# Two-layer graph attention on one core: a scores group, a combination group and the multiplications with the inverses change their places

## The chip, the cores and the metric

The kernel runs on one core of a Trainium2 chip. The metric is the device time of one launch in microseconds (us), a median of runs. A core has five engines, each with its own queue of instructions: the matrix engine (PE), the vector engine (DVE), the scalar engine (ACT), GpSimd (POOL) and the sync engine (SP), which here only issues transfers (DMA). The engines run beside each other and wait for each other by semaphores. PE writes its results to the accumulation memory PSUM[...]; DVE and ACT read them from there.

## The reference, cut to what matters

64 graphs of 256 nodes with 512 features go through two layers. Each layer normalises, applies ReLU and masked multi-head attention, and adds the result to its input.

```python
# layer 0: 4 heads of 64 (Wq, Wk, Wv, Wo), adj masks the scores
h = relu(layernorm(x));  x = x + attention0(h, adj)
# layer 1: layernorm once more inside, 8 heads of 64 (w_qkv, w_out), mask = adj | eye
h = relu(layernorm(x));  x = x + attention1(layernorm(h) * gamma + beta, adj)
# attention: softmax(where(mask, q k^T / 8, very negative)) v, then the output projection and a bias
```

All is in float32.

## The kernel before

`fast_path` takes the graphs two at a time: 32 steps, each with 512 rows (NT = 4 tiles of 128 rows). A head pair (two heads of 64, 128 columns) of one layer is a **unit**; layer 0 has the units (0,0) and (0,1), layer 1 has (1,0) to (1,3). Layer 1 takes them in the order 0, 2, 1, 3.

What one unit does, with the lines that the profile names:

- **scores** (PE, L742): q k^T, transposed, for two heads and two graphs into four PSUM tiles `sc`. DVE adds the mask (L750), which also frees the PSUM tile; ACT takes the exponential (L751); POOL adds the two halves of the keys (L752).
- **weigh** (PE, L763): the exponentials times v into one `sc` tile `po`, and the sums of the exponentials (L773) into another. DVE takes the reciprocal of the sums (L778, two instructions), and SP spreads the inverses over the partitions with eight transfers (L784). `inv` and `invb` have one buffer each.
- **normalise** (DVE): `po` times the inverses (L799), and a check of the range (L800). These two free the tiles `po` and `sums`.

The pool of `sc` tiles has four buffers. So a scores group, which takes all four, waits for the L799 and L800 of the weighing before it, and a weighing that directly follows a scores group waits for the first two L750 of that group. The pool `mm` for all other PE results has four buffers as well.

Around the units lie the projections: q and k (L654; `project_qk`, by seven products of half size instead of eight, evacuated in `evacuate` by L598 to L610), v of layer 0 (`project_v0`, L678, four groups, evacuated by ACT's L682) and v of layer 1 (L692). `combine0` (L703, four groups, added to x by DVE's L707) and `combine1` (L717, seven groups, evacuated in `accumulate` by L617 to L632, with POOL's L620, L621 and L626) are the output projections. `norm1` takes row statistics (L523, L524), the negative mean (L563), ReLU on ACT (L564) and the statistics of that; `norm0` takes the statistics of layer 0's input; `row_scales` makes the scale (POOL L531) and shift (DVE L532) from them. `transpose_h` turns a normalised tile on PE (L581), evacuated by ACT (L585 in layer 0, L587 in layer 1); `act_sums` forms the four sums that the seven products need on POOL (L396 to L399). The load of the next h (L467) has one buffer and follows the transposes of the h before it.

**The order.** Steps are laid over each other: in one period PE does layer 1 of step s, the middle of step s+1 and the projections of layer 0 of step s+2. Every piece of work is entered with a time by hand, `at(period, place, ...)`; a period is 6.1 of these units. The pieces are then recorded in the order of their times. On PE this recorded order is the program's order (`manual_schedule` for PE alone). The order of the instructions on DVE, ACT, POOL and SP is set by a scheduler at build time, which takes the recorded order as one of its inputs. [...]

`attend` enters a unit: its scores at `place`, its weighing at `weighed` (plus a thousandth), its normalise some time later.

Of the kernel before, what the change touches and what calls it, by code (L numbers as in the profile page):

```python
# [315 lines left out]
def fast_path(  # L316
# [498 lines left out]
    def at(period, place, fn, *args):  # L815
        events.append((period * PERIOD + place, len(events), fn, args))

    def at_set(period, place, share, fn, *args):
        for i, n in enumerate((1, 6, 7, 5, 2, 4, 3)):
            at(period, place + i * share / 7, fn, *args, n)  # L820

    def attend(period, place, s, lyr, pr, later, weighed, first, last):

        at(period, place, scores, s, lyr, pr)
        at(period + later, weighed + 0.001, weigh, s, lyr, pr)
        at(period + later, weighed + 0.3, normalise, s, lyr, pr, first, last)

    for s in range(NSTEP):

        p = s - 2  # L830
        at(p - 1, 5.7, load_h, s)
        at(p, 0.2, adjacency_cast, s)
        for t in range(NT):
            at(p, 0.4 + 0.4 * t, norm0, s, t)
            at(p, 2.05 + 0.2 * t, scale_row, s, t)
        at(p, 2.4, adjacency_turn, s)
        at(p, 2.75, masks, s)
        for c in range(NC):
            at(p, 3.03 + 0.03 * c, transpose_h, s, 0, c)
        at_set(p, 3.57, 1.0, project_qk, s, 0, 0)  # L840
        for t in range(NT):
            at(p, 4.57 + 0.14 * t, project_v0, s, t)
        attend(p, 4.85, s, 0, 0, 0, 5.7, True, False)
        attend(p, 5.7, s, 0, 1, 1, 1.0, False, True)
        p = s - 1
        at(p, 1.4, load_x, s)
        at(p, 2.6, first_bias, s)
        for t in range(NT):
            at(p, 3.0 + 0.14 * t, combine0, s, t)
            at(p, 3.5 + 0.25 * t, norm1, s, t)  # L850
            at(p, 4.5 + 0.1 * t, scale_row, s, t)

        for c in range(NC):
            at(p, 5.13 + 0.02 * c, transpose_h, s, 1, c)
        p = s
        at_set(p, 0.0, 1.0, project_qk, s, 1, 0)
        at_set(p, 1.0, 1.0, project_v1, s)
        at_set(p, 2.0, 1.0, project_qk, s, 1, 1)
        attend(p, 1.0, s, 1, 0, 0, 2.1, True, False)
        attend(p, 2.1, s, 1, 2, 0, 3.0, False, False)  # L860
        attend(p, 3.0, s, 1, 1, 0, 3.6, False, False)
        attend(p, 3.6, s, 1, 3, 0, 4.2, False, True)
        at_set(p, 5.2, 0.9, combine1, s)
        at(p, 6.1, store, s)
# [12 lines left out]
def kernel(tc, *args):  # L877
    nc = tc.nc
    B, N, _ = args[0].shape
    P = 128  # L880
    with tc.tile_pool(name="guard", bufs=1) as guard:
        extremes = guard.tile([P, B // 2 * 6], FP, name="extremes")
        ident = guard.tile([P, P], FP, name="ident")
        make_identity(nc, ident)
        fast_path(tc, *args, ident, extremes)
        safe = guard.tile([1, 1], I32, name="safe")
        with tc.tile_pool(name="gps", bufs=1, space=bass.MemoryType.PSUM) as ps:
            top = guard.tile([P, 1], FP, name="top")
            nc.vector.tensor_reduce(top, extremes, axis=mybir.AxisListType.X, op=ALU.max)
            row = ps.tile([1, P], FP, name="row")  # L890
            nc.tensor.transpose(row, top, ident)
            all_top = guard.tile([1, 1], FP, name="all_top")
            nc.vector.tensor_reduce(all_top, row, axis=mybir.AxisListType.X, op=ALU.max)
            nc.vector.tensor_scalar(safe, all_top, LIMIT, None, op0=ALU.is_le)
        flag = nc.values_load(safe[0:1, 0:1], min_val=0, max_val=1, skip_runtime_bounds_check_because="a comparison gives 0 or 1")
        with tc.If(flag < 1):
            general_path(tc, *args)
# [29 lines left out]
```

## Time and profile before

| | |
|---|---|
| time, median of 3 runs | 3617.09 us (3614.64 to 3617.94) |
| profiled execution, span on the core | 3612.3 us |
| granted TensorE clock, mean | 0.989 |
| bytes moved by DMA | 165.45 MB, 46 GB/s in the mean |
| inverses, L784 | 1536 transfers of 32 KB, 1.8 us each from issue to landing |
| DVE waits for the inverses (L799) | 546.3 us in 165 waits |

The page sums the busy time of each engine and gives its share of the span. Since instructions of different engines overlap, these shares don't add up to anything; what counts is which engine is hardly ever idle, and what it waited for when it was. In a list of waits each line names who waited, for whom, and then the total, the number and the longest of the waits in microseconds. In a timeline each line gives the start, the length, the engine, the source line, the operation, output and input tiles and the number of merged instructions; a bracket at the end gives the idle time before it and what ended it. Matmuls in float32 appear twice per instruction of the program: 16 records of L742 are one scores group of 8.

### The profile page before, as it was taken

What the parts mean: (1) busy time and instruction counts of PE and PEld (TensorE: products, weight loads), DVE (VectorE), ACT (ScalarE), POOL (GpSimd) and SP (SyncE); (2) the same over time, 40 slices, a digit from 0 to 9 for tenths busy, and PEclk for the clock granted to TensorE, in tenths of its full rate; (3) what the DMA queues carried; (4) which work ended last, traced back from release to release, by engine and by line L of the source; (5) the groups of instructions that cost most, each with busy time, mean ns of one, the idle gap of its engine ahead of it and who ended that gap; (6) DMA issues with size and microseconds to landing.
All of it is one profiled execution on the core that took longest, in us unless ns stands there. A gap on an engine that the chain in (4) does not pass through costs nothing.

```text
span 3612.3 us, 51508 instructions
## 1 busy us (share of the span) xinstructions
PE 3473.9 (96%) x19555; PEld 2653.3 (73%) x19586; DVE 2068.4 (57%) x3873; ACT 1146.8 (32%) x1873; POOL 1652.7 (46%) x1387
## 2 busy tenths in 40 slices
PE   5999999999999999999999999999999999999987
PEld 4777777777777777777777777777777777777765
DVE  4555565565565556555566555565655565655553
ACT  2333333333332333232333333333333332333321
POOL 4445444454444455444545444544444554445432
PEclk8999999999999999999999999999999999999998
DMA  4011111111111111111111111111111111111100
GB/s 134 24 49 52 28 42 50 50 51 33 44 45 50 49 51 29 42 49 52 50 52 29 42 50 50 52 38 42 40 51 50 50 30 42 49 50 50 39 27 24
DMA packets 146956, 165.45 MB, mean 46 GB/s; under 512 B 43272, under 2 KB 94992, under 8 KB 146704
## 3 DMA queue, kind: packets, MB, share of 16 engines
q1 hardware_dynamic: 141312, 155.30, 14.1%
q10 hardware_dynamic: 5392, 6.82, 0.6%
q8 instruction: 155, 2.54, 0.3%
q14 instruction: 97, 0.79, 0.1%
HBM read 78.12 MB, written 33.55 MB: 31 GB/s over the span
## 4 chain that ended last, share of the span: by engine, by line
PE 67%; DVE 12%; DMA 8%; SPq 8%; issue 2%; ACT 1%; POOL 0%; DVEq 0%; POOLq 0%
PE mm L654 23%; PE mm L692 11%; SPq L784 8%; PE sc L742 8%; PE sc L763 7%; PE mm L703 5%; PE mm L717 5%; DMA h<-in_x_dram 4%; DMA invb<-inv 4%; DVE inv L778 3%; PE mm L678 3%; DVE bs L523 2%; PE sc L773 2%; DVE p L750 2%; PE mm L581 2%
## 5 line engine op out<-in xcount | busy, mean ns | idle before, releaser
L752 POOL TENSOR_TENSOR pd<-p 128x512 f32<-128x512 f32 x384 | 479.0, 1269 | 777.5 <-PE sc L773 732.8
L654 PE MATMUL mm<-hT,wqkv 128*128 128x256 f32 x3584 | 804.3, 381 | 1.6
L654 PEld LDWEIGHTS mm<-hT,wqkv 128*128 128x128 f32 x3584 | 676.0, 190 | 105.7 <-issue 13.5
L751 ACT ACTIVATE p<-p 128x512 f32<-128x512 f32 x768 | 464.1, 630 | 572.4 <-DVE p L750 570.5
L750 DVE TENSOR_TENSOR p<-sc,n 128x512 f32<-128x512 f32 x768 | 481.0, 680 | 154.7 <-PE sc L742 150.0
L742 PE MATMUL sc<-qk 64*128 64x256 f32 x3072 | 415.1, 395 | 34.6 <-DVE oT L799 25.9
L799 DVE TENSOR_TENSOR oT<-sc,invb 128x512 f32<-128x512 f32 x192 | 132.6, 691 | 547.2 <-DMA invb<-inv 546.3
L717 PE MATMUL mm<-wo,oT 128*128 128x256 f32 x1792 | 405.5, 384 | 18.5 <-POOL oT L397 13.1
L654 PE MATMUL mm<-hT,wqk 128*128 128x256 f32 x1792 | 409.0, 383 | 1.2 <-issue 1.2
L763 PE MATMUL sc<-p,v 128*64 128x256 f32 x3072 | 375.5, 386 | 29.3 <-DVE p L750 26.9
L692 PE MATMUL mm<-wqkv,hT 128*128 128x256 f32 x1792 | 400.6, 381 | 0.0
L654 PEld LDWEIGHTS mm<-hT,wqk 128*128 128x128 f32 x1792 | 335.8, 190 | 82.9 <-issue 40.8
L742 PEld LDWEIGHTS sc<-qk 64*128 64x128 f32 x3072 | 287.4, 187 | 148.0 <-issue 63.1
L717 PEld LDWEIGHTS mm<-wo,oT 128*128 128x128 f32 x1792 | 338.6, 192 | 76.6 <-POOL oT L397 14.2
L778 DVE RECIPROCAL inv<-sc 128x128 f32<-128x128 f32 x384 | 338.8, 923 | 83.3 <-PE sc L773 79.9
L692 PEld LDWEIGHTS mm<-wqkv,hT 128*128 128x128 f32 x1792 | 338.0, 190 | 57.6 <-issue 13.1
L480 POOL TENSOR_TENSOR xt<-xt,bo_b 128x512 f32<-128x512 f32 x128 | 161.4, 1292 | 466.1 <-DMA xt<-in_x_dram 327.9
L763 PEld LDWEIGHTS sc<-p,v 128*64 128x64 f32 x3072 | 211.2, 137 | 187.1 <-DVE p L750 83.0
L703 PE MATMUL mm<-wo,oT 128*128 128x512 f32 x512 | 235.8, 603 | 19.5 <-DVE oT L799 19.5
L538 ACT ACTIVATE h<-h,mr,r 128x512 f32<-128x512 f32 x256 | 187.5, 802 | 208.4 <-DVE mr L532 208.4
L678 PE MATMUL mm<-wv,hT 128*128 128x256 f32 x1024 | 243.9, 393 | 0.0
L523 DVE BATCH_NORM_STATS2 bs<-h 128x6 f32<-128x512 f32 x256 | 171.3, 680 | 99.3 <-ACT h L564 54.7
(105 smaller groups left out, 3375.7 us busy)
## 6 DMA issues: line engine op xcount, KB each, us to landing
invb<-inv SPq DMA_DIRECT2D x1536, 32.0 KB, 1.8
h<-in_x_dram SPq DMA_DIRECT2D x32, 1024.0 KB, 5.1
xt<-in_x_dram SPq DMA_DIRECT2D x32, 1024.0 KB, 5.1
out_dram<-xt SPq DMA_DIRECT2D x32, 1024.0 KB, 4.3
ad<-in_adj_dram SPq DMA_DIRECT2D x32, 128.0 KB, 2.2
wr<-in_L_gnn_w_qkv_dram ACTq DMA_DIRECT2D x3, 1024.0 KB, 8.2
wr<-in_L_gnn_w_out_dram ACTq DMA_DIRECT2D x1, 1024.0 KB, 8.7
wqk<-in_L_gnn_Wq_dram ACTq DMA_DIRECT2D x4, 128.0 KB, 4.9
```

The costliest lines, as they stand in the source:

```text
L654: nc.tensor.matmul(bank[:, k, :], w[:, wa, c, k, a * P:(a + 1) * P], st["hT"][:, ba, c, :], start=first and (k, c) == (0, 0), stop=(k, c) ...
L678: nc.tensor.matmul(bank, st["hT"][:, b0 + t // NIC * step, c % HC, i:i + P], wv0[:, c, :], start=(c == 0), stop=(c == NC - 1),)
L692: nc.tensor.matmul(bank[:, t, :], st["hT"][:, ba, c, t * P:(t + 1) * P], wqkv1[:, wa, c, 2, :], start=first and (t, c) == (0, 0), stop=(t, ...
L703: nc.tensor.matmul(bank, st["oT0"][:, pr, t // NIC, t % NIC * P:(t % NIC + 1) * P], wo0[:, pr, :], start=(pr == 0), stop=(pr == PR0 - 1),)
L717: nc.tensor.matmul(bank[:, t, :], st["oT1"][:, ba, c, t * P:(t + 1) * P], wo1[:, wa, c, :], start=first and (t, c) == (0, 0), stop=(t, c) ...
L742: nc.tensor.matmul(sc[e, g][:, kc, :], qk[rows, 1, k0:k0 + P], qk[rows, 0, g * N:(g + 1) * N], start=True, stop=True,)
L750: nc.vector.tensor_tensor(p[e][:, g], sc[e, g], neg[:, :, g, :], ALU.add)
L751: nc.scalar.activation(p[e][:, g], p[e][:, g], AF.Exp, scale=SCALE)
L752: nc.gpsimd.tensor_tensor(pd[:, e], p[e][:, :, 0, :], p[e][:, :, 1, :], ALU.add)
L763: nc.tensor.matmul(po[e * DH:(e + 1) * DH, g, :], st[f"v{lyr}"][:, g * NIC + kc, c0:c0 + DH], p[e][:, g, kc, :], start=(kc == 0), stop=(kc ...
L778: nc.vector.reciprocal(inv[:, i * P:(i + 1) * P], sums[:, i * P:(i + 1) * P])
L784: nc.sync.dma_start(invb[d0:d0 + 32, g, :], inv[r0:r0 + 32, :])
```

## The change

Three kinds of places move.

- The scores of unit (0,0) are entered at 5.0 instead of 4.85. The four groups of `project_v0` stand at 4.57, 4.71, 4.85 and 4.99, so the scores now follow all four; before they stood between the third and the fourth (in some early steps between the second and the third). The weighing of (0,0) and the scores of (0,1) go from 5.7 to 5.75, and thereby behind the fifth group of `combine1` (5.714) instead of the fourth. This is meant to give the L799 of unit (1,3), which frees two of the `sc` tiles, more time.
- The first group of `combine0` is entered at 3.01 instead of 3.0, and thereby behind the weighing of unit (1,2) at 3.001. Before it stood between the scores of (1,1) and that weighing. The three other groups follow after the transposes, as before. This is meant to bring that weighing and its inverses forward.
- `normalise` is entered 0.5 behind its weighing instead of 0.3, except for the last unit of a layer in a step. This is meant to let other DVE work go ahead of a multiplication that would have to wait for its inverses.

The same instructions are executed with the same operands.

```diff
@@ attend
         at(period, place, scores, s, lyr, pr)
         at(period + later, weighed + 0.001, weigh, s, lyr, pr)
-        at(period + later, weighed + 0.3, normalise, s, lyr, pr, first, last)
+        at(period + later, weighed + (0.3 if last else 0.5), normalise, s, lyr, pr, first, last)
@@ for s in range(NSTEP), p = s - 2
             at(p, 4.57 + 0.14 * t, project_v0, s, t)
-        attend(p, 4.85, s, 0, 0, 0, 5.7, True, False)
-        attend(p, 5.7, s, 0, 1, 1, 1.0, False, True)
+        attend(p, 5.0, s, 0, 0, 0, 5.75, True, False)
+        attend(p, 5.75, s, 0, 1, 1, 1.0, False, True)
@@ p = s - 1
         for t in range(NT):
-            at(p, 3.0 + 0.14 * t, combine0, s, t)
+            at(p, 3.01 + 0.14 * t, combine0, s, t)
             at(p, 3.5 + 0.25 * t, norm1, s, t)
```

## The prediction

> **What bounds the kernel now.** First the busy times on the page: the matrix engine (PE) is busy nearly all the time, so every place where PE stands still is worth its length, and other work only what it makes PE wait.
>
> ```profile
> span 3612.3 us, 51508 instructions
> ...
> PE 3473.9 (96%) x19555; PEld 2653.3 (73%) x19586; DVE 2068.4 (57%) x3873; ACT 1146.8 (32%) x1873; POOL 1652.7 (46%) x1387
> ```
>
> Then the list of waits, PE alone. After the prologue two waits recur in almost every step:
>
> ```profile
> PE sc L763 <- DVE p L750: 26.9, 30, 1.5
> PE sc L742 <- DVE oT L799: 25.9, 27, 3.1
> ```
>
> Then one typical step in the timeline, PE first (start, length, line, in brackets the idle time before it):
>
> ```profile
> 1821.32 1.13 PE L742 MATMUL sc<-qk 64*128 64x256 f32 x8
> 1822.83 1.13 PE L742 MATMUL sc<-qk 64*128 64x256 f32 x8 [0.37 <-DVE qk L610]
> 1823.89 1.98 PE L703 MATMUL mm<-wo,oT 128*128 128x512 f32 x4
> 1825.80 1.95 PE L763 MATMUL sc<-p,v 128*64 128x256 f32 x16
> ...
> 1838.96 1.95 PE L763 MATMUL sc<-p,v 128*64 128x256 f32 x16
> ...
> 1859.78 1.14 PE L742 MATMUL sc<-qk 64*128 64x256 f32 x8
> 1861.72 1.47 PE L742 MATMUL sc<-qk 64*128 64x256 f32 x8 [0.80 <-DVE oT L799]
> 1863.12 1.99 PE L678 MATMUL mm<-wv,hT 128*128 128x256 f32 x8
> 1864.95 1.91 PE L581 MATMUL mm<-ident,h 128*128 128x128 f32 x16
> 1866.70 7.07 PE L717 MATMUL mm<-wo,oT 128*128 128x256 f32 x32
> 1873.70 2.00 PE L742 MATMUL sc<-qk 64*128 64x256 f32 x16
> 1876.50 1.95 PE L763 MATMUL sc<-p,v 128*64 128x256 f32 x16 [0.80 <-DVE p L750]
> ```
>
> (Units are written (layer, head pair).) An undisturbed scores group takes 1.93 us. The one at 1859.78 (layer 0, pair 0) takes 3.34, so PE loses 1.40; over the 28 steady steps the mean is also 1.40. The weighing at 1876.50 comes 0.87 late, 1.00 in the mean. The weighing at 1838.96 comes on time: the mean loss there is 0.1. The rest of the step runs without gaps. Last VectorE (DVE) and GpSimd (POOL) at the same places:
>
> ```profile
> 1836.65 0.68 DVE L799 TENSOR_TENSOR oT<-sc,invb 128x512 f32<-128x512 f32 x1
> ...
> 1838.19 1.29 DVE L750 TENSOR_TENSOR p<-sc,n 128x512 f32<-128x512 f32 x2 [0.18 <-PE sc L742]
> 1839.40 0.68 DVE L523 BATCH_NORM_STATS2 bs<-h 128x6 f32<-128x512 f32 x1
> ```
>
> ```profile
> 1875.44 1.26 POOL L626 TENSOR_TENSOR xt<-xt,u 128x512 f32<-128x512 f32 x1
> 1878.46 1.02 POOL L531 TENSOR_TENSOR r<-ve,mhalf 128x4 f32<-128x4 f32 x1 [1.76 <-DVE ve L550]
> ```
>
> [...] DVE stood 5.57 us before L799 at 1860.98 for a transfer, and the L750s behind it followed only then. [...] The trace shows 3.4 us stretches at half clock, each 1.7 us lost, right after the scores waits of steps near 655, 1532, 2846 and 3395, whose longest gaps were 1.50 to 1.80; gaps of 1.54 and 1.64 went unpunished. [...]
>
> **The change part by part.** Only places move, and nothing is computed more or less. Because only PE follows the recorded order and a scheduler orders the others, I read the built order of each engine before and after; 28 steady steps are alike.
>
> (B) *Scores of layer 0, pair 0, behind the whole v projection.* They wait for two PSUM buffers held by the weighing of unit (1,3) until its L799 and L800. Now the fourth v group (1.83 us, 1863.12 to 1864.95) goes first. L800 ended at 1862.00; scores would start at 1859.78 + 1.83 = 1861.61 and need the second pair of buffers 1.06 later. Gain 1.40 per step, less 0.05 for late transfers: 30 x 1.35 = 40 us, and about 8 us of half clock behind these waits: -48.
>
> (A) *First combine0 group behind the weighing of unit (1,2).* Weighing and sums (2.45) end at 1826.34 instead of 1828.25. The weighing now follows its scores directly, but the first L750 (1.24 after the scores' start, 0.68 long) is done just in time, as elsewhere, so at most 0.07 appears. The two L778 start 0.14 later and take 1.77: done at 1828.25. From there to L799 are eight transfers: 6.35 and 7.1 us in this step's other units, mostly 6.5, mean 6.7. L799 is ready at 1834.75, and the change of 0.3 to 0.5 does not keep it back: in the new DVE order it stands directly behind the third L707 (end 1834.66), where before it stood behind the fourth. Worse, the statistics of the third h row (L523 at 1839.40, between the L750s) now stand *ahead of* all L750s of scores (1,3), and they hang on a chain DVE, ACT, DVE. Step lengths from the trace: L799 and L800 0.93; L523 0.61; L707 0.59; L524 0.11; L523 of xt 0.73; L524 0.22; L563 to ACT's L564 0.19; L564 0.75; L523 0.60: L750 starts 4.73 later, at 1839.48, and the weighing of (1,1), which needs that PSUM buffer, 0.77 later at 1840.25 instead of 1838.96. Queued behind it are all of PE's matmuls. Cost 1.3 with 6.5, 1.2 to 1.9 with the two ends, mean 1.5 - 0.1 = 1.4: +42 us in 30 steps. It is not given back: the later reciprocals move by 0.8 to 1.0, and scores (0,0) have that much slack now.
>
> (C, D) *Behind the moved scores.* Call their start 0. By the undisturbed scores at 1805.31, L750s start from 1.24 and ACT's L751s at 1.96, 2.56, 3.16. ACT's new order is three L751, the first L587, the fourth L751, three L587 (before: all L751 long done). So the first L587 runs 3.76 to 4.53, and the first L717, whose PSUM buffer it frees, starts at 4.57 instead of 1.93 + 1.75 = 3.68: C = 0.89. Five L717 groups, not four, now stand ahead of scores (0,1): 4.57 + 5 x 1.75 + 1.93 = 15.25 for the weighing (0,0). It needs the first L750 of scores (0,1). In the new DVE order this stands behind L532, which needs POOL's L531 (before, two of these L750s ran at 1875.77, ahead of L550). POOL starts its first L752 behind the third L751 at 3.85, then eight more instructions 1.23 apart (L752, L396 to L399, L620, L621, L626), so L531 starts at 14.92, takes 1.02, L532 some 0.1, and the L750 starts at 16.07; weighing at 16.84: D = 1.59. Counted from the transposes' start that is 14.91 against 11.68 now, of which 1.75 is the group moved ahead: +1.48 together, whatever the split. Were POOL free earlier, L550 (14.2) would set L531, and D would be 1.0; L532 beside a POOL instruction took 1.23 instead of 0.16[...]; here POOL is idle behind L531, so I take 0.1. 30 x 1.48 = +45, ends +27 and +60.
>
> *Other multiplications recorded later* ((1,0), (1,1), (0,0)): no PE wait lies near them and two VectorE evacuations move ahead of the one of (0,0), hidden behind the projection: 0. Prologue +-2, tail unchanged in DVE order: 0.
>
> (E) *Half clock.* Gaps of 1.3 and 1.6 lie at the lower edge of those that were punished. Unknown; from 0 to 1.7 us for each D and four A in ten (70 us). I take one step in six: 5 x 1.7 = +8.
>
> Sum: -48 + 42 + 45 + 8 = +47: 3617 + 47 = 3664 us.
>
> **Rivals.** (1) As worked out, 3664. (2) Each new gap trips the clock: without E +39, and 30 x 1.7 x 0.9 = +46: 3702. For it: 1.50 was once enough; against: 1.64 once was not. (3) The gain of B stands and the new waits are hidden, because transfers, POOL or ACT are quicker than I chain them: 3617 - 48 = 3569. For it: B's wait is plain in the trace; against: the step lengths vary by hardly 0.1 us from step to step, and the orders are fixed. (4) One of A and C+D is real, the other is not: -48 + 43 = -5: 3612, no change.
>
> **How the numbers follow.** (1) 0.66, (2) 0.15, (3) 0.14, (4) 0.05. Slower 0.81, the same 0.05, faster 0.14. Below 3610 lies case 3, above 3710 some 0.05: the range 3610 to 3710 leaves out 0.19.
>
> **What would show it.** Right: the L742 wait for L799 shrinks to a few us; L763 waits for L750 at two places per step, about 60 times and over 80 us in all; a new wait of L717 for ACT's L587 of 0.9 us; POOL's L531 directly behind L626 with no idle time. Wrong: if the weighing of (1,1) starts on time, A falls; if L717 starts directly behind the transposes, C falls; if POOL idles before L531, D is nearer 1.0; more than eight half-clock stretches in the steady part mean rival 2.

## The result and the profile after

| | before | after |
|---|---|---|
| median of 4 runs | 3615.86 us (3614.05 to 3617.94) | 3665.11 us (3661.97 to 3670.33) |
| ratio to before, with its 95% interval | | 1.0137 (1.0120 to 1.0155) |
| profiled span | 3612.3 us | 3665.8 us |
| granted TensorE clock, mean | 0.989 | 0.987 |
| mean step, 27 steady steps | 109.66 us | 111.66 us |

The change makes the kernel 49 us slower. One wait went, and two others came or grew. From the page of the kernel after, span and busy times:

```profile
span 3665.8 us, 51478 instructions
...
PE 3465.2 (95%) x19555; PEld 2649.2 (72%) x19586; DVE 2091.5 (57%) x3873; ACT 1124.1 (31%) x1873; POOL 1654.7 (45%) x1387
```

PE shows the same 19555 records and is busy for 9 us less; the span is 53 us longer. What was added is idle time of PE. The list of waits of PE, after (total, number, longest, in us):

```profile
PE sc L763 <- DVE p L750: 101.4, 60, 2.8
...
PE mm L717 <- ACT hT L587: 13.1, 25, 0.5
...
PE sc L742 <- DVE oT L799: 1.7, 4, 0.9
```

The wait of the scores for L799 went from 25.9 us to 1.7: the change did what it was for. The wait of weighings for L750 went from 26.9 us in 30 waits to 101.4 in 60, that is, from one place in a step to two, and each is longer. L717's wait for L587 is new. Both places are seen in one step of PE's timeline, after (start, length, ..., idle time before it):

```profile
1858.52 2.00 PE L742 MATMUL sc<-qk 64*128 64x256 f32 x16
1861.64 1.95 PE L763 MATMUL sc<-p,v 128*64 128x256 f32 x16 [1.13 <-DVE p L750]
...
1884.20 2.64 PE L742 MATMUL sc<-qk 64*128 64x256 f32 x16
1886.77 1.97 PE L581 MATMUL mm<-ident,h 128*128 128x128 f32 x16
1888.84 8.90 PE L717 MATMUL mm<-wo,oT 128*128 128x256 f32 x40
1897.67 2.00 PE L742 MATMUL sc<-qk 64*128 64x256 f32 x16
1902.21 3.60 PE L763 MATMUL sc<-p,v 128*64 128x256 f32 x16 [2.54 <-DVE p L750]
```

The scores of (1,3) at 1858.52 are followed by a gap of 1.13 ahead of the weighing of (1,1): place A of the prediction. The scores of (0,0) at 1884.20 no longer have a gap inside (place B); in this step they take 2.57 to the next group, 0.64 more than undisturbed. From the start of the transposes L581 to that of L717 pass 2.07 us instead of 1.75 (C; in a typical step 2.51). Behind the scores of (0,1) a gap of 2.54 stands ahead of the weighing of (0,0) (D), and that weighing then takes 3.60 instead of 1.95, because PE ran at half clock (from 1902 to 1906 its granted clock was 0.57 in the mean).

Why at A: DVE's timeline of the same step, after.

```profile
1856.22 0.69 DVE L799 TENSOR_TENSOR oT<-sc,invb 128x512 f32<-128x512 f32 x1
...
1860.31 0.69 DVE L523 BATCH_NORM_STATS2 bs<-h 128x6 f32<-128x512 f32 x1 [0.79 <-ACT h L564]
1860.92 2.46 DVE L750 TENSOR_TENSOR p<-sc,n 128x512 f32<-128x512 f32 x4
```

L799 of unit (1,2) is followed by statistics and an evacuation of other rows, then by the L523 of the third h row, which waits 0.79 for ACT. Only then come the four L750. The first scores tiles had been complete since about 1859.76 (1.24 after the start, as in the prediction); the L750 that frees the tile starts 1.16 later, and PE's gap there is 1.13. That the L523 causes this is read from the trace; no run moved it alone.

Why at C: ACT's timeline, after.

```profile
1886.29 1.83 ACT L751 ACTIVATE p<-p 128x512 f32<-128x512 f32 x3 [1.61 <-DVE p L750]
1888.02 0.76 ACT L587 ACTIVATE hT<-mm,gb 128x512 f32<-128x512 f32 x1
```

The first L587, which frees the tile that the first L717 writes to, runs behind three exponentials and ends at 1888.78; the L717 starts at 1888.84.

Why at D: POOL's timeline and then DVE's, after.

```profile
1889.16 2.50 POOL L752 TENSOR_TENSOR pd<-p 128x512 f32<-128x512 f32 x2
...
1899.10 1.29 POOL L626 TENSOR_TENSOR xt<-xt,u 128x512 f32<-128x512 f32 x1
1900.32 1.04 POOL L531 TENSOR_TENSOR r<-ve,mhalf 128x4 f32<-128x4 f32 x1
```

```profile
1898.76 0.43 DVE L550 TENSOR_SCALAR ve<-mv 128x4 f32<-128x4 f32 x1
1901.39 0.16 DVE L532 SCALAR_TENSOR_TENSOR mr<-mv,r 128x4 f32<-128x4 f32 x1 [2.20 <-POOL r L531]
1901.47 2.48 DVE L750 TENSOR_TENSOR p<-sc,n 128x512 f32<-128x512 f32 x4
```

L531 has no bracket: it runs directly behind L626, at the end of an unbroken row of POOL work. L550, its input, had been ready since 1899.19. DVE therefore stands 2.20 us before L532, with the L750 of scores (0,1) queued behind it until 1901.47, though the first scores tiles had been complete since about 1898.91 (1.24 after the start), and PE stands with it.

### The profile page after: what moved, and what is told of

It reads as the page before. It is cut to its first block, busy times and chain, and to the rows that moved or that the text cites. A ratio compares the mean times of both kernels' runs of the same rounds, so it can differ in the third digit from the quotient of the medians.

```text
span 3665.8 us, 51478 instructions
## 1 busy us (share of the span) xinstructions
PE 3465.2 (95%) x19555; PEld 2649.2 (72%) x19586; DVE 2091.5 (57%) x3873; ACT 1124.1 (31%) x1873; POOL 1654.7 (45%) x1387
## 4 chain that ended last, share of the span: by engine, by line
PE 73%; DVE 10%; SPq 5%; POOL 4%; DMA 3%; ACT 3%; issue 2%; DVEq 0%; POOLq 0%; ACTq 0%
PE mm L654 27%; PE mm L692 11%; PE sc L763 10%; PE mm L717 9%; PE sc L742 6%; PE mm L678 5%; SPq L784 5%; PE sc L773 3%; DMA invb<-inv 3%; DVE inv L778 2%; DVE bs L523 2%; DVE p L750 2%; ACT p L751 1%; DVE oT L799 1%; POOL r L531 1%
## 5 line engine op out<-in xcount | busy, mean ns | idle before, releaser
L752 POOL TENSOR_TENSOR pd<-p 128x512 f32<-128x512 f32 x384 | 479.4, 1271 | 888.0 <-PE sc L773 750.7
L750 DVE TENSOR_TENSOR p<-sc,n 128x512 f32<-128x512 f32 x768 | 476.5, 681 | 176.8 <-PE sc L742 173.4
L751 ACT ACTIVATE p<-p 128x512 f32<-128x512 f32 x768 | 456.0, 628 | 351.2 <-DVE p L750 308.8
L763 PE MATMUL sc<-p,v 128*64 128x256 f32 x3072 | 387.3, 395 | 104.5 <-DVE p L750 101.4
L717 PE MATMUL mm<-wo,oT 128*128 128x256 f32 x1792 | 412.3, 388 | 30.4 <-ACT hT L587 13.1
L717 PEld LDWEIGHTS mm<-wo,oT 128*128 128x128 f32 x1792 | 341.0, 193 | 98.1 <-ACT hT L587 20.7
L742 PE MATMUL sc<-qk 64*128 64x256 f32 x3072 | 395.4, 392 | 6.7 <-DVE qk L610 3.5
L763 PEld LDWEIGHTS sc<-p,v 128*64 128x64 f32 x3072 | 215.6, 140 | 256.2 <-DVE p L750 143.9
L799 DVE TENSOR_TENSOR oT<-sc,invb 128x512 f32<-128x512 f32 x192 | 132.7, 691 | 449.8 <-DMA invb<-inv 448.7
L742 PEld LDWEIGHTS sc<-qk 64*128 64x128 f32 x3072 | 280.1, 186 | 108.7 <-issue 55.1
L703 PE MATMUL mm<-wo,oT 128*128 128x512 f32 x512 | 235.6, 603 | 19.5 <-DVE oT L799 19.5
L678 PE MATMUL mm<-wv,hT 128*128 128x256 f32 x1024 | 226.2, 379 | 0.0
L523 DVE BATCH_NORM_STATS2 bs<-h 128x6 f32<-128x512 f32 x256 | 171.5, 681 | 92.6 <-ACT h L564 69.4
```

What stands on the lines that cost most here:

```text
L523: nc.vector.bn_stats(bs, src[:, t, :])
L678: nc.tensor.matmul(bank, st["hT"][:, b0 + t // NIC * step, c % HC, i:i + P], wv0[:, c, :], start=(c == 0), stop=(c == NC - 1),)
L703: nc.tensor.matmul(bank, st["oT0"][:, pr, t // NIC, t % NIC * P:(t % NIC + 1) * P], wo0[:, pr, :], start=(pr == 0), stop=(pr == PR0 - 1),)
L717: nc.tensor.matmul(bank[:, t, :], st["oT1"][:, ba, c, t * P:(t + 1) * P], wo1[:, wa, c, :], start=first and (t, c) == (0, 0), stop=(t, c) ...
L742: nc.tensor.matmul(sc[e, g][:, kc, :], qk[rows, 1, k0:k0 + P], qk[rows, 0, g * N:(g + 1) * N], start=True, stop=True,)
L750: nc.vector.tensor_tensor(p[e][:, g], sc[e, g], neg[:, :, g, :], ALU.add)
```

## The experiments

What the runs measured, place by place: mean loss per step over the 27 steady steps of each trace (the stretch of PE less what it takes undisturbed: 1.93 for scores, 1.75 for the transposes), and the stretches at half clock that begin between 200 and 3400 us (3.4 us each; one in the kernel before and two in `after_room` last 6.8).

| kernel | B | A | C | D | half clock | median us | ratio to before |
|---|---|---|---|---|---|---|---|
| before | 1.35 | 0.11 | 0 | 0.99 | 6 | | 1 |
| after | 0.13 | 1.57 | 0.68 | 2.01 | 9 | 3665.11 | 1.0137 |
| combine_only | 1.15 | 1.51 | 0 | 0.95 | 5 | 3645.86 | 1.0101 |
| scores_weigh | 0.14 | 0.06 | 0.66 | 2.04 | 9 | 3630.15 | 1.0050 |
| scores_only | 0.17 | 0.09 | 0.65 | 0.41 | 0 | 3569.51 | 0.9886 |
| between | 0.13 | 0.12 | 0.66 | 0 | 0 | 3563.33 | 0.9866 |
| after_short | 0.11 | 1.52 | 0.68 | 1.12 | 2 | 3630.71 | 1.0073 |
| between_514 | 0.03 | 0.12 | 0.15 | 0 | 0 | 3539.40 | 0.9813 |
| after_between | 0.12 | 1.52 | 0.68 | 0 | 2 | 3602.09 | 0.9983 |
| after_room | 2.69 | 1.17 | 1.04 | 1.97 | 30 | 3751.33 | 1.0396 |

The first four experiments ran beside a before of 3611.89 us, the others beside one of 3607.97, so kernels are compared by their ratios. A D of 0 means that the weighing doesn't wait; the L717 group that then stands alone ahead of it takes 0.16 more than one in a row, which D doesn't count. One edit got no run: with the later `normalise` alone, the built order of the instructions on all five engines is that of the kernel before, and taking it out of the kernel after leaves its order too as it was. That edit does nothing.

**One part alone: the combination group (`combine_only`).**

```diff
-            at(p, 3.0 + 0.14 * t, combine0, s, t)
+            at(p, 3.01 + 0.14 * t, combine0, s, t)
```

> The kernel before with the combine0 places at 3.01 alone. Theory (the four terms of the prediction are separate and add up): only term A appears, the weighing of (1,1) waits for the first L750 of scores (1,3) by 1.3 to 1.6 us a step, while the scores wait for L799 at layer 0 stays at 1.4 and the late weighing of (0,0) at 1.0: 3617 + 31 x 1.45 = about 3662 us, +1.2%. Rival (A is only the shadow of the moved scores of layer 0, which shift the vector engine's work of the next step): no wait at (1,1), 3617 us within 6 us. Rival 2 (the earlier inverses of (1,2) bring all later units forward, so that part of A comes back at the scores of layer 0): the L799 wait shrinks to below 0.5 and the time is about 3630.

Measured: 3645.86 us (3642.96 to 3650.92), ratio 1.0101 (1.0084 to 1.0117), so +34 us, less than expected. A appears in full, 1.51. But the loss at B shrank from 1.35 to 1.15, and in two of the 27 steps to nothing. PE's waits, `combine_only`:

```profile
PE sc L763 <- DVE p L750: 68.6, 60, 2.5
PE sc L742 <- DVE oT L799: 23.0, 23, 3.1
```

A wait put in early in the step takes a little from a wait late in the step. The prediction had said that A is not given back; here, where B still stands, 0.2 of it is. In the kernel after, where B is gone, there is nothing left to give. The mean step is 1.00 us longer than before: A's 1.41 and 0.22 of half clock behind it stand against 0.41 less at B and in the half clock behind B. Another 0.15 goes to PE's order alone: with the moved group in its new place, PE takes 1.82 instead of 1.91 from the start of that L703 to the next group and 1.75 instead of 1.80 for the transposes, in every step and without a wait.

**The other part alone: scores, weighing and scores of layer 0 (`scores_weigh`).**

```diff
-        attend(p, 4.85, s, 0, 0, 0, 5.7, True, False)
-        attend(p, 5.7, s, 0, 1, 1, 1.0, False, True)
+        attend(p, 5.0, s, 0, 0, 0, 5.75, True, False)
+        attend(p, 5.75, s, 0, 1, 1, 1.0, False, True)
```

> The kernel before with the places 5.0 and 5.75 of the two layer-0 units alone. Theory: terms B, C and D without A: -48 + 30 x 1.75 (C and D as the changed kernel shows them, 0.76 + 1.99 against 1.00) + some 12 us of half clock = 3617 + 17 = 3634 us, and together with the kernel above it adds up to the change. By the prediction's own sizes it would be 3617 - 48 + 45 + 8 = 3622. Rival (the gain of B holds by itself, C and D come from the shift that A makes): below 3590.

Measured: 3630.15 us (3624.05 to 3633.90), ratio 1.0050 (1.0033 to 1.0067): +18 us, near what was expected. PE's waits, `scores_weigh`:

```profile
PE sc L763 <- DVE p L750: 57.2, 30, 2.5
...
PE mm L717 <- ACT hT L587: 12.4, 24, 0.5
```

30 waits, one per step, all at D; A isn't there. The two parts alone cost 34 + 18 = 52 us, both together 49: they add up.

**The scores moved, and nothing else (`scores_only`); the weighing moved as well, but not scores (0,1) (`between`).**

```diff
# scores_only
-        attend(p, 4.85, s, 0, 0, 0, 5.7, True, False)
+        attend(p, 5.0, s, 0, 0, 0, 5.7, True, False)
# between
-        attend(p, 4.85, s, 0, 0, 0, 5.7, True, False)
+        attend(p, 5.0, s, 0, 0, 0, 5.75, True, False)
```

> The kernel before with the scores of (0,0) at 5.0, but the weighing of (0,0) and the scores of (0,1) left at 5.7, so four L717 groups and not five stand ahead of scores (0,1). The vector engine's order then keeps two of its L750 ahead of L550 and L532. Theory: B is gained, C (0.76) appears, but the weighing of (0,0) is then bound by the load of h as before and is no later than before, counted from the transposes, so C is taken out of the old 1.0: 3617 - 48 + 5 = 3574 us, -1.2%. Rival (the loss of C and D comes from scores that stand directly ahead of the transposes, whatever follows): C + D again 2.7, 3617 - 48 + 52 + 10 = 3631.

> The kernel before with the scores of (0,0) at 5.0 and its weighing at 5.75, but the scores of (0,1) left at 5.7: the fifth L717 group now stands between the scores of (0,1) and the weighing of (0,0). Theory: B is gained; the 1.75 us of that group cover the wait of the weighing for its L750, so D goes to nothing and only C (0.76) stays: 3617 - 48 - 30 + 23 = 3562 us, -1.5%. Rival (L628 behind L532 now comes late and holds the PSUM bank that the next projection needs): a new wait of L654 for L628 or L630 of about 1 us a step, 3592.

Measured: 3569.51 us (3568.84 to 3570.68), ratio 0.9886 (0.9869 to 0.9902), and 3563.33 us (3561.79 to 3564.61), ratio 0.9866 (0.9850 to 0.9882). Both are faster than before by 42 and 49 us. So the idea behind the scores' move is sound. C stays in both (0.65); the larger harm, D, lies in one further place: that the scores of (0,1) follow five `combine1` groups instead of four. With four, D is 0.41 or nothing, and no steady step of either kernel runs at half clock.

**POOL's queue shortened within the change (`after_short`).** Two of POOL's additions in the output projection of layer 1 are left out (which leaves out part of that projection's result); all else is the kernel after.

```diff
-            nc.gpsimd.tensor_tensor(r12, r12, u, ALU.add)
-            nc.gpsimd.tensor_tensor(r21, r21, u, ALU.add)
+            pass
+            pass
```

> The changed kernel without POOL's L620 and L621 (two of the additions of u, so part of the output projection of layer 1 is left out); the vector engine's order is the same. Theory (D is set by the chain of POOL instructions in front of L531): two times 1.23 us fall out of the chain, L531 then follows L550 and starts some 0.75 to 0.95 us earlier, D falls from 2.0 to about 1.1 and the half-clock stretches behind it go: 3665 - 27 - 12 = about 3626 us. Rival (D is set by the vector engine, the statistics of the late h and L628 in front of L550, POOL is only released by it): no change, 3665 us.

Measured: 3630.71 us (3629.68 to 3635.73), ratio 1.0073 (1.0056 to 1.0090). D fell from 2.01 to 1.12. POOL's timeline, then DVE's, `after_short`:

```profile
1879.28 1.27 POOL L626 TENSOR_TENSOR xt<-xt,u 128x512 f32<-128x512 f32 x1 [0.46 <-DVE xt L625]
1881.17 1.02 POOL L531 TENSOR_TENSOR r<-ve,mhalf 128x4 f32<-128x4 f32 x1 [0.62 <-DVE ve L550]
```

```profile
1882.23 0.16 DVE L532 SCALAR_TENSOR_TENSOR mr<-mv,r 128x4 f32<-128x4 f32 x1 [1.13 <-POOL r L531]
1882.31 2.48 DVE L750 TENSOR_TENSOR p<-sc,n 128x512 f32<-128x512 f32 x4
```

Now POOL idles before L531 and waits for L550. So POOL's queue had set D, and L550 sets it once POOL is quicker, near the 1.0 that the prediction gave for that case. Seven of nine half-clock stretches went with it.

**The scores behind the first transposes (`between_514`).** A try for the best version: `between`, with the scores of (0,0) one place later, so that the first L587 may go ahead of their exponentials.

```diff
-        attend(p, 4.85, s, 0, 0, 0, 5.7, True, False)
+        attend(p, 5.14, s, 0, 0, 0, 5.75, True, False)
```

> The kernel before with the scores of (0,0) at 5.14, that is behind the first of the four transpose groups L581, its weighing at 5.75, and the scores of (0,1) at 5.7. Theory (C is the exponentials in front of the first L587 on ACT, and nothing else): now the first L587 stands in front of the exponentials, the first L717 finds its PSUM bank free, C is gone too: the 3563 us of the kernel with the scores at 5.0 less 30 x 0.75 = 3541 us, -2.0% against before. Rival (C comes back at the second L717 group, which waits for the second L587, now behind three exponentials): 3563.

Measured: 3539.40 us (3537.30 to 3539.71), ratio 0.9813 (0.9797 to 0.9829): 69 us faster than before, and the fastest of all. ACT's, DVE's and PE's timelines, `between_514`:

```profile
1821.81 0.78 ACT L587 ACTIVATE hT<-mm,gb 128x512 f32<-128x512 f32 x1
1823.59 1.83 ACT L751 ACTIVATE p<-p 128x512 f32<-128x512 f32 x3 [1.00 <-DVE p L750]
```

```profile
1835.31 1.25 DVE L750 TENSOR_TENSOR p<-sc,n 128x512 f32<-128x512 f32 x2
1836.48 0.31 DVE L550 TENSOR_SCALAR ve<-mv 128x4 f32<-128x4 f32 x1
1837.92 0.16 DVE L532 SCALAR_TENSOR_TENSOR mr<-mv,r 128x4 f32<-128x4 f32 x1 [1.13 <-POOL r L531]
```

```profile
1821.17 0.60 PE L581 MATMUL mm<-ident,h 128*128 128x128 f32 x4
1821.70 2.00 PE L742 MATMUL sc<-qk 64*128 64x256 f32 x16
1823.63 1.53 PE L581 MATMUL mm<-ident,h 128*128 128x128 f32 x12
1825.00 7.07 PE L717 MATMUL mm<-wo,oT 128*128 128x256 f32 x32
1832.00 2.00 PE L742 MATMUL sc<-qk 64*128 64x256 f32 x16
1833.93 1.99 PE L717 MATMUL mm<-wo,oT 128*128 128x256 f32 x8
1835.85 1.95 PE L763 MATMUL sc<-p,v 128*64 128x256 f32 x16
```

The first L587 runs before the L751s: C is gone but for 0.15, as the divided transposes take a little longer. The L750s stand ahead of L550 and L532: D is gone, although DVE still waits 1.13 us before L532, since nothing that PE needs at once is queued behind it. PE runs through without a bracket.

**D taken out of the change (`after_between`).** The kernel after, with the scores of (0,1) back at 5.7.

```diff
-        attend(p, 5.75, s, 0, 1, 1, 1.0, False, True)
+        attend(p, 5.7, s, 0, 1, 1, 1.0, False, True)
```

> The changed kernel with the scores of (0,1) back at 5.7, so that the fifth L717 group stands between them and the weighing of (0,0). Theory: D goes (the changed kernel loses 2.0 and some half-clock stretches there), A and C stay: 3563 of the kernel without the moved combine0 group, plus A, 31 x 1.45 to 1.5 = 3608 us, about as fast as before. Rival (A is partly given back, as the kernel with that move alone, +34, suggests): 3597. That give-back needs a wait at the scores of layer 0 to be spent on, which this kernel has not, so I expect the larger number.

Measured: 3602.09 us (3595.73 to 3605.63), ratio 0.9983 (0.9976 to 0.9990). Against the kernel after this is 1.54% of the time, about 56 us, for one place in PE's order. The mean step falls by 2.19: 2.02 at D and 0.37 in the half clock behind it, less the 0.16 that a lone L717 group costs. Against `between`, which lacks only A, the ratios differ by 1.17%, about 42 us: the price of A once B is gone. B is the same in both (0.12 and 0.13), so nothing of A is given back there, as expected.

**Room at A (`after_room`): a miss.** The kernel after, with the scores of (1,3) and the weighing of (1,1) one projection group later, so that the late L750 of A would be hidden.

```diff
-        attend(p, 3.0, s, 1, 1, 0, 3.6, False, False)
-        attend(p, 3.6, s, 1, 3, 0, 4.2, False, True)
+        attend(p, 3.0, s, 1, 1, 0, 3.72, False, False)
+        attend(p, 3.72, s, 1, 3, 0, 4.2, False, True)
```

> The changed kernel with the scores of (1,3) and the weighing of (1,1) at 3.72 instead of 3.6, behind one more projection group (1.82 us), so that the chain of statistics in front of L750 has ended when the scores come. Theory: A falls from 1.5 to about 0.3; but the reciprocals of (1,1), now behind L570 and L532, start later against PE by 2.5 to 3 us, which is more than the 1.2 us of slack at the scores of layer 0, so a wait for L799 of 1.3 to 1.7 us comes back there: 3665 us within 12. Rival (the slack is enough): 3665 - 36 = 3629.

Measured: 3751.33 us (3740.83 to 3755.86), ratio 1.0396 (1.0373 to 1.0419), 2.6% above the kernel after and far above what was expected. DVE's timeline, `after_room`, and then the scores of (0,0) on PE:

```profile
1904.68 0.70 DVE L523 BATCH_NORM_STATS2 bs<-h 128x6 f32<-128x512 f32 x1 [0.79 <-ACT h L564]
1905.29 0.68 DVE L600 TENSOR_TENSOR qk<-mm,qk 128x512 f32<-128x512 f32 x1
...
1906.55 1.27 DVE L750 TENSOR_TENSOR p<-sc,n 128x512 f32<-128x512 f32 x2
...
1911.66 1.22 DVE L532 SCALAR_TENSOR_TENSOR mr<-mg,r 128x4 f32<-128x4 f32 x1 [1.13 <-POOL r L531]
1912.80 1.76 DVE L778 RECIPROCAL inv<-sc 128x128 f32<-128x128 f32 x2
...
1920.89 0.69 DVE L799 TENSOR_TENSOR oT<-sc,invb 128x512 f32<-128x512 f32 x1 [5.00 <-DMA invb<-inv]
...
1930.71 0.69 DVE L799 TENSOR_TENSOR oT<-sc,invb 128x512 f32<-128x512 f32 x1 [5.58 <-DMA invb<-inv]
```

```profile
1931.46 2.41 PE L742 MATMUL sc<-qk 64*128 64x256 f32 x8 [2.22 <-DVE oT L799]
```

Two things happened. The scheduler used the room: the L523 of the h row now comes before the first scores tiles are complete, but an evacuation and the statistics of another row stand between it and the first L750, so A shrank only to 1.17 in the mean. And the reciprocals of (1,1) stand behind L532, which waits for POOL: they start at 1912.80, though the sums that they read were done about 1909.8. `inv` and `invb` have one buffer, so this delay runs through both chains of transfers to the L799 at 1930.71, and the scores of (0,0) wait again, longer than in the kernel before: B is 2.69. The direction was expected, the size was not. 30 half-clock stretches, 21 more than in the kernel after, lose about 1.7 us each, the two long ones twice that: some 39 of the some 90 us, in part already within B's 2.69.

## Why the prediction was right

Forecast 3664, measured 3665.1, for the reasons that were given; that the sum came so close is in part luck. Per step the forecast was +1.57 (47 us in 30 steps), and the 27 steady steps measured +2.00. Cut at each group, PE's timeline gives this as -1.53 at B, +1.53 at A, +2.21 at C and D, each with the half clock behind it, and -0.20 around the moved `combine0` group, of which the forecast had nothing. The steady steps make 54 us. The steps ahead of them got 3 us faster instead of slower, since the kernel before lost up to 3.9 us at B there, and the end 3 us slower. Term by term:

- **B, -48.** The loss fell from 1.35 to 0.13 (0.05 forecast), 1.22 x 30 = 37 us, and of the six half-clock stretches, all of which followed gaps of L742, none is left there: 6 x 1.7 = 10. The four v groups, no longer divided, also take 7.00 instead of 7.10. Right.
- **A, +42.** The loss rose by 1.46 in the mean (1.4 forecast); 42 us by `after_between` against `between`. Mechanism and size right. Given-back time is nil in the kernel after, but not in general, as `combine_only` shows.
- **C, 0.89.** Typically 0.84 (0.76 longer transposes and 0.08 in L717), in the mean 0.76, because where the scores start late, part of C vanishes in that. A little too large. In the list of waits it is only 0.5 long each time, as that list counts from the modelled end of the transposes, which without a wait overlaps the next matmul by 0.16 (1864.95 + 1.91 against 1866.70 in the kernel before).
- **D, 1.59.** 2.01 in the mean, 1.88 typically; the step that was mis-sized. Part of it is only C's complement: counted from the transposes' start, C and D together were forecast as 14.91 to the weighing, and are 15.15 in the median step, 15.05 at the least. The rest is in single steps: the first L752 starts late where L799 of (1,3) is late, since POOL does the sums of oT (L397 to L399) first, and the whole row of POOL work shifts. In the step shown above the third L751 ended at 1888.12, 3.92 after the scores' start (3.85 forecast), but L399 still ran until 1889.20, and L752 started only then. The row itself was right: `after_short` shortened it, and D fell.
- **C and D together, +45.** The net rise is 1.78 per step in the mean (1.48 forecast): 53 us in 30 steps.
- **E, +8.** Nine half-clock stretches instead of six, all behind L763 rather than L742. The prediction said that more than eight would mean rival 2. As a sign this was set too low: nine stretches of 1.7 us are 15 us, where rival 2 needed 46. In number it was one step in three, not in six, so this term too was mis-sized.
- **Normalise, 0.** The price was right, the reason partly not: the evacuation that moves ahead of L799 of (0,0) does so because of the move of the weighing to 5.75 (it is ahead in `between`, and behind in `scores_only`), and the edit alters no engine's order.

Rival 3 (the gain of B stands, 3569 us) is near what `between` measures, 3563, where C is still in and D is gone altogether. It fails in the kernel after by A and D. Rival 4 falls, as both A and D are real.

## What to carry to other kernels

A group moved in PE's order to end one wait also moves the work that it feeds and the work that it stood ahead of; read the built order of every engine behind the move, and ask of each instruction that PE needs which waiting instruction is queued ahead of it. Here the move of the scores of (0,0) alone gained 42 us, 49 with the weighing of (0,0), and one place for the scores of (0,1) cost 56. Where an engine must wait for a slow neighbour, as DVE does at L532, the better cure is not a shorter wait but nothing urgent behind it: with a wait of 1.13, `after_short` still loses 1.12 at D, and `between_514` nothing.

## What the runs showed of the hardware

How often a gap of PE brought on 3.4 us at half clock depended on its length. Pooled over the ten traces above, from 200 to 3400 us: after gaps of 0.25 to 1.5 us, 0 of some 500; from 1.5 to 2.0 us, 19 of 86; from 2.0 to 2.5 us, 19 of 31; above 2.5 us, 25 of 31.

The granted clock in each trace that has several half-clock stretches shows all of them starting on one grid of 3.413 us, to within 0.005 us, wherever the gaps lie. Sorted by the idle time of PE inside one interval of that grid at full clock, half clock followed 0 of 9189 intervals with less than 1.5 us, 19 of 69 with 1.5 to 2.0 us, and all 44 with more. A long gap that the grid divided could go unpunished: in the kernel after, the gap of 2.82 us at 1190.72 had 1.49 in one interval and 1.34 in the next, and no half clock followed. What decides between 1.5 and 2.0 us stays open.

Beyond its length, a wait with half clock behind it cost about 1.7 us, estimated as half of the 3.41 us that the stretch lasted (the weighing at 1902.21 in the kernel after took 1.65 more than an undisturbed one), and twice that in the three of 63 cases where the half clock lasted 6.8 us. So in these kernels the first microseconds cut from a wait of 2.5 us were worth more than the last, as in `after_short`, where D fell from 2.01 to 1.12 and seven of nine stretches went.
